# A graph-attention kernel: other PSUM grouping, later row sums of squares, three adjacency tiles turned early, and PE busy until x comes

## The chip, the cores and the metric

The kernel runs on one core of one Trainium2 chip. The time is the device time of one execution in microseconds. Before the change it is 2200.85 us, the median of 3 runs (2199.65 to 2201.54). The profiled execution spans 2198.8 us.

## The reference

There are 16 images (B) of 1024 nodes (N) with 256 channels (C), and one adjacency matrix of 1024 x 1024 for all. All is float32. Cut to what matters:

```python
fea = transpose(x, (0, 2, 1)); c_adj = mean(fea, axis=1)              # a mean per node
diff = c_adj[:, None, :] - c_adj[:, :, None]
A = abs(abs(sigmoid(diff) - 0.5) - 0.5) * 2.0                         # likeness of two nodes
g = relu(einsum('bcn,bnm->bcm', fea, adj * (A + A^T) / 2) * para)     # queries: a graph product
k, v = x @ kv_w                                                       # keys, values, 4 heads of 64
x = layernorm(x + softmax(q k^T * scale) v)
h = relu(x @ w1_loop + adj @ (x @ w1_neigh) + b1)                     # two graph convolutions
h = relu(h @ w2_loop + adj @ (h @ w2_neigh) + b2)
x = layernorm(x + (x + h) / 2)
```

## The kernel before

One function writes the order of the work by hand, engine by engine: within `tc.manual_schedule()` each engine runs its instructions in the order in which `run()` (L834) calls them, and waits only where a tile is not yet written, or where a buffer is still in use. Image by image, `run()` overlaps four things: the attention of image b, the query graph of image b+1, and the two graph convolutions of images b-1 and b-2.

**Attention** (L495). Four units (two pairs of heads, two halves of the nodes). `scores` makes eight tiles of 128 x 1024 with PE, takes the exponential of each on ScalarE (ACT, L519) and adds the eight up on VectorE (DVE, L525). `outputs` multiplies them with the values; `add` divides and adds the result onto x in a blocked layout (`xB`).

**Query graph.** For the first two images, `Queries` (L367) loads a row of adjacency tiles, weighs it by the likeness (two ACT passes, one DVE pass) and runs eight steps of plain matmuls. From the third image on, `FastQueries` (L410) makes the 2 x 2 block product from seven products instead of eight. `step` (L456) runs over four k; at k = 0 it takes three PSUM tiles of two banks each ("big") and one bank, and gives the seven sums their places: products 1 and 6 share tile a, 7 and 5 tile b, 2 and 3 tile c, and 4 has the single bank. In the last step they are finished in the order 1, 6, 2, 7, 4, 5, 3. `end` (L475) combines them: ACT copies product 1 (L482), then DVE makes seven additions (L483 to L489), two multiplications by para (L491), and ACT two relus (L492).

**Keys and values** of the next image follow on PE at once: `keys` (L342) takes two big PSUM tiles, one after the other, and ACT copies each to kT (L352); `values` (L355) takes four single banks in turn, and ACT copies each to v (L364). There are three big tiles and two single banks in all, and scores use the big ones as well. Between the two halves of the keys stands one small matmul (L256) that sums the squares over channels, for the variance.

**The norm after attention** is `BlockedNorm` (L301). `mean` subtracts the mean of each node (L312), `squares` squares on ACT (L318), sums over 32 channels on DVE (L319) and joins the two halves (L260). `variance` (L322) makes the small matmul, scales on DVE (L324) and takes the power -1/2 on GpSimd (L326). `scale` (L328) and `spread` (L333) multiply and transpose on DVE and store the nodes. In the steady image the calls are: step 2 of the query graph, with `mean` and `squares` inside it, step 3, `end`, the keys with `variance` between their halves, `scale`, `spread`, the values.

**The transposed adjacency.** The convolutions need the transposed matrix. `adj_blocked` (L204) loads a tile in blocks of 32 x 32 with four DMAs of small pieces, and `turn_adj` (L864) transposes it in two halves on DVE (L871) into tiles that stay in SBUF, or, for the upper right quarter, into row buffers (`rows01`) that are stored to DRAM later. All eight tiles are loaded and turned within image 1's query graph (b = 0). Row buffers (`row_tile`, L99) are 23 of 128 x 1024, shared by nearly everything.

**The start.** x of image 0 is loaded in four pieces; `prepare_first` (L219) transposes them on PE as they come (L227), then follow the keys, a row of means, the values, and the query graph of image 0, whose fifth step (t = 4) also prepares image 1 on DVE: its transposes and the sums for its means.

Of the kernel before, what the change touches and what calls it, by code (L numbers as in the profile page):

```python
# [18 lines left out]
def kernel(  # L19
# [31 lines left out]
    nc = tc.nc  # L51
# [39 lines left out]
    def bank_psum(name):  # L91
        return psum.tile([P, FB], F32, tag="bank", name=name, bufs=2)
# [6 lines left out]
    def row_tile(name):  # L99
        return work.tile([P, N], F32, tag="row", name=name, bufs=ROWS)  # L100

    def load_blocked(b, name):
        tiles = []
        for cc in range(NC):
            t = row_tile(f"xB_{name}_{cc}")
            for a in range(Q):
                c0 = cc * P + a * S
                nc.sync.dma_start(
                    out=t[a * S:(a + 1) * S, :].rearrange("k (bn r) -> k bn r", r=S),
                    in_=x[b, :, c0:c0 + S].rearrange("(bn k) r -> k bn r", k=S))  # L110
            tiles.append(t)
        return tiles
# [185 lines left out]
    def by_node(t):  # L298
        return t.rearrange("p (bn r) -> p bn r", r=S)

    class BlockedNorm:  # L301
# [10 lines left out]
                nc.vector.tensor_sub(x_cc, x_cc, mean.unsqueeze(2).to_broadcast([P, NB, S]))  # L312

        def squares(self):
            self.part = small.tile([P, NC, NB], F32, tag="part", name=f"sq_part_{self.name}", bufs=2)
            for cc in range(NC):
                sq = row_tile(f"sq_{self.name}_{cc}")
                nc.scalar.activation(sq, self.xB[cc], AF.Square)  # L318
                nc.vector.tensor_reduce(self.part[:, cc, :], by_node(sq), AX.X, ALU.add)  # L319
            join(self.part)  # L320

        def variance(self):  # L322
# [44 lines left out]
    class Queries:  # L367
# [35 lines left out]
        def end(self):  # L403
            qT = work.tile([P, NC, N], F32, tag="qT", name=f"qT_{self.b}")
            for cb in range(NC):
                nc.vector.tensor_mul(qT[:, cb, :], self.pg[cb], para_sb[:, cb, :])
                nc.scalar.activation(qT[:, cb, :], qT[:, cb, :], AF.Relu, scale=QSCALE)  # L407
            return qT

    class FastQueries(Queries):  # L410
# [45 lines left out]
        def step(self, k, halfway=None):  # L456
            if k == 0:
                a, b, c = (big_psum(f"g_ps_{self.b}_{i}") for i in range(3))
                h0, h1 = ts(0, FB), ts(1, FB)
                self.p = {1: a[:, h0], 6: a[:, h1], 7: b[:, h0], 5: b[:, h1], 2: c[:, h0], 3: c[:, h1],  # L460
                          4: bank_psum(f"g_ps_{self.b}_3")}
            lo, hi = self.wg.pop(k), self.wg.pop(TJ + k)
            t12, t4 = self.T.pop(k)
            h0, h1 = ts(0, FB), ts(1, FB)
            terms = {1: (self.block(0, 0), lo[:, h0]), 2: (self.block(0, 1), hi[:, h0]), 3: (self.S[3], hi[:, h1]),
                     4: (self.block(1, 1), t4), 5: (self.S[0], t12[:, h0]), 6: (self.S[1], t12[:, h1]),
                     7: (self.S[2], lo[:, h1])}

            for n in (1, 6, 2, 7, 4, 5, 3) if k == TJ - 1 else (1, 2, 3, 5, 7, 6, 4):
                if n == 7 and halfway:  # L470
                    halfway()
                x_n, w_n = terms[n]
                nc.tensor.matmul(self.p[n], x_n[:, k, :], w_n, start=(k == 0), stop=(k == TJ - 1))  # L473

        def end(self):  # L475
            qT = work.tile([P, NC, N], F32, tag="qT", name=f"qT_{self.b}")
            u = row_tile(f"U_{self.b}")
            h0, h1 = ts(0, FB), ts(1, FB)
            p = self.p
            add = nc.vector.tensor_add  # L480
            p1 = row_tile(f"P1_{self.b}")[:, h0]
            nc.scalar.copy(p1, p[1])  # L482
            add(u[:, h0], p1, p[6])  # L483
            add(qT[:, 0, h0], p1, p[2])
            add(u[:, h1], u[:, h0], p[7])
            add(qT[:, 1, h0], u[:, h1], p[4])
            add(qT[:, 1, h1], u[:, h1], p[5])
            add(u[:, h0], u[:, h0], p[5])
            add(qT[:, 0, h1], u[:, h0], p[3])  # L489
            for cb in range(NC):  # L490
                nc.vector.tensor_mul(qT[:, cb, :], qT[:, cb, :], para_sb[:, cb, :])  # L491
                nc.scalar.activation(qT[:, cb, :], qT[:, cb, :], AF.Relu, scale=QSCALE)  # L492
            return qT

    class Attention:  # L495
# [46 lines left out]
        def add(self, u):  # L542

            b, (pair, j) = self.b, UNITS[u]
            half = FB // S
            pd = bank_psum(f"den_ps_{b}_{u}")
            den = pd[:, 0:2 * half]
            nc.tensor.matmul(den, fold.rearrange("p a k -> p (a k)"), self.part.pop(u), start=True, stop=True)
            rden = small.tile([P, half], F32, tag="rden", name=f"rden_{b}_{u}", bufs=2)
            for s in range(2):  # L550
                rows = slice(s * HD, (s + 1) * HD)
                nc.vector.reciprocal(rden[rows, :], den[rows, ts(s, half)])
            nc.vector.tensor_tensor(den_min, den_min, den, ALU.min)
            nc.vector.tensor_tensor(den_max, den_max, den, ALU.max)
            o = by_node(self.o.pop(u))
            nc.vector.tensor_mul(o, o, rden.unsqueeze(2).to_broadcast([P, half, S]))
            dst = by_node(self.xB[pair][:, ts(j, FB)])
            nc.vector.tensor_add(dst, dst, o)
            nc.vector.tensor_reduce(self.sums[:, pair, ts(j, half)], dst, AX.X, ALU.add)
            if u == len(UNITS) - 1:  # L560
                join(self.sums)
# [272 lines left out]
    def run():  # L834
# [3 lines left out]

        xT, c_col = prepare_first(x_first)
        q = Queries(0, x_first)
        for t in range(NT):
            q.load(t)
        load_para()
        blocked = load_blocked(1, "1")
        load_weights()

        def first_weights():
# [7 lines left out]
        for t in (1, 2):  # L857
            q.times_adj(t)
        xb = load_x(1, "1")
        tiles = {}  # L860

        rows01 = []

# [9 lines left out]
        for t in range(NT):  # L873
            if t + 3 < NT:
                q.weigh(t + 3)
            q.step(t)
            if t == 4:
                xB = load_blocked(0, "a0")
                ready = {}
                ready["xT"], ready["part"] = prepare(blocked, "1")  # L880
            if t == 6:
                ready["mean"] = means(ready["part"], "1")
        qT = q.end()
        convs = {}
        for b in range(B):
# [84 lines left out]
            if more and not c1:  # L970
                xT = ready["xT"]
                for t in range(3, NT):
                    q.load(t)
                for t in range(3, NT):
                    q.likeness(t)
                for mt in range(4):
                    tiles[mt] = adj_blocked(mt)
                q.times_adj(3)
                q.step(0)
                q.times_adj(4)  # L980
                q.step(1)
                att.add(3)
                for mt in range(4, NT):
                    tiles[mt] = adj_blocked(mt)
                q.times_adj(5)
                q.step(2)
                q.step(3)
                norm.mean()
                q.times_adj(6)
                q.times_adj(7)  # L990
                q.step(4)
                norm.squares()
                q.step(5)
                q.step(6)
                norm.variance()
                xB = load_blocked(b + 1, f"a{b + 1}")
                q.step(7)
                qT = q.end()
                norm.scale()
                norm.spread()  # L1000
                turn_adj(range(NT))
                kT, v = keys(b + 1, xT), values(b + 1, xT)
            elif more:
                xT = ready["xT"]
                q.pair(2)
                q.step(0)
                q.step(1, lambda: att.add(3))
                q.pair(3)
                q.step(2, lambda: (norm.mean(), norm.squares()))
                q.step(3)  # L1010
                qT = q.end()
                xB = load_blocked(b + 1, f"a{b + 1}")
                kT = keys(b + 1, xT, norm.variance)
                norm.scale()
                norm.spread()
                v = values(b + 1, xT)
            else:
                c2.load_h1()
                c2.load_x()
                both.fetch(2, 3)  # L1020
                c1.inner()
                both.left(nc.gpsimd)
                both.fetch(1, 4)
                both.run({1: (lambda: att.add(3),), 2: (norm.mean, norm.squares), 7: (norm.variance,),
                          5: (norm.scale, norm.spread)})
                c1.turn(0)
                c2.last()
                c1.turn(1)
# [85 lines left out]
```

## Time and profile before

| what | value |
|---|---|
| time, median of 3 | 2200.85 us |
| span of the profiled execution | 2198.8 us |
| PE busy | 2172.8 us (99%) |
| DVE busy | 1864.0 us (85%) |
| ACT busy | 969.3 us (44%) |
| GpSimd busy | 328.1 us (15%) |
| DMA moved | 258.59 MB, mean 118 GB/s |
| mean granted TensorE clock | 0.997 |
| one image in the steady part | some 134.7 us |

Busy shares say what an engine did, not what it cost; idle time of an engine that nobody waits for costs nothing. In the timeline a row has the start in us, the length in us, the engine, the line, the operation, and what it writes and reads; several equal instructions in a row are merged, with their number after the x. In brackets stands the idle time of the engine before it and what ended it. In the waits, a row has the waiting engine and line, what it waited for, and the total, the number and the longest wait. A matmul of the program shows as two records on PE. PE is TensorE, PEld its weight loads.

### The profile page before, as it was taken

What the parts mean: (1) busy time and instruction counts of PE and PEld (TensorE: products, weight loads), DVE (VectorE), ACT (ScalarE), POOL (GpSimd) and SP (SyncE); (2) the same over time, 40 slices, a digit from 0 to 9 for tenths busy, and PEclk for the clock granted to TensorE, in tenths of its full rate; (3) what the DMA queues carried; (4) which work ended last, traced back from release to release, by engine and by line L of the source; (5) the groups of instructions that cost most, each with busy time, mean ns of one, the idle gap of its engine ahead of it and who ended that gap; (6) DMA issues with size and microseconds to landing.
All of it is one profiled execution on the core that took longest, in us unless ns stands there. A gap on an engine that the chain in (4) does not pass through costs nothing.

```text
span 2198.8 us, 22720 instructions
## 1 busy us (share of the span) xinstructions
PE 2172.8 (99%) x8096; PEld 1032.4 (47%) x8096; DVE 1864.0 (85%) x2453; ACT 969.3 (44%) x1064; POOL 328.1 (15%) x177
## 2 busy tenths in 40 slices
PE   8998999999999999999999999999999999999997
PEld 4344444544444444444444445445454444544354
DVE  4988888888898988988889788998989889888965
ACT  4734445434454443545444454434544445434511
POOL 1000020210302103021030301203012020210021
PEclk9999999999999999999999999999999999999999
DMA  8294372633646335463453734527264272733342
GB/s 193 86 139 148 60 182 68 124 125 63 177 100 151 104 58 172 96 172 88 75 162 78 182 86 78 172 58 182 86 92 157 58 182 88 137 114 64 116 134 97
DMA packets 586359, 258.59 MB, mean 118 GB/s; under 512 B 488064, under 2 KB 552448, under 8 KB 586240
## 3 DMA queue, kind: packets, MB, share of 16 engines
q1 hardware_dynamic: 585968, 256.56, 48.4%
q8 instruction: 65, 1.06, 0.2%
q14 instruction: 54, 0.44, 0.1%
q10 hardware_dynamic: 272, 0.52, 0.1%
HBM read 210.90 MB, written 46.14 MB: 117 GB/s over the span
## 4 chain that ended last, share of the span: by engine, by line
PE 72%; DVE 24%; issue 2%; ACT 1%; DMA 0%; DVEq 0%; SPq 0%; POOLq 0%; ACTq 0%; POOL 0%
PE hu_ps L793 16%; PE s L516 15%; PE av L536 15%; DVE acc L525 6%; PE k_ps L350 5%; PE v_ps L362 5%; PE t_ps L634 3%; PE h_ps L700 2%; PE hu_ps L641 2%; PE g_ps L400 2%; PE h_ps L701 2%; DVE wg L392 2%; DVE sq_part L319 1%; DVE wg L446 1%; DVE T L445 1%
## 5 line engine op out<-in xcount | busy, mean ns | idle before, releaser
L519 ACT ACTIVATE pr<-s 128x1024 f32<-128x1024 f32 x512 | 476.1, 1052 | 179.5 <-PE s L516 179.1
L525 DVE TENSOR_TENSOR acc<-acc,pr 128x1024 f32<-128x1024 f32 x384 | 493.2, 1285 | 41.4 <-DVE acc L525 0.9
L516 PE MATMUL s<-qT,kT 64*128 64x512 f32 x2048 | 457.2, 596 | 0.7 <-ACT qT L407 0.7
L536 PE MATMUL av<-pr,v 128*64 128x512 f32 x2048 | 453.6, 595 | 0.0
L516 PEld LDWEIGHTS s<-qT,kT 64*128 64x128 f32 x2048 | 190.9, 186 | 236.5 <-ACT pr L519 114.8
L536 PEld LDWEIGHTS av<-pr,v 128*64 128x64 f32 x2048 | 141.4, 137 | 300.0 <-issue 289.7
L326 POOL TENSOR_TENSOR rstd<-rstd,neg_half 128x32 f32<-128x32 f32 x16 | 87.1, 5441 | 1149.9 <-DVE rstd L324 1149.9
L386 ACT ACTIVATE wg<-c_row,c_col 128x1024 f32<-128x1024 f32 x128 | 147.1, 1149 | 86.5 <-DVE accB L527 50.6
L392 DVE SCALAR_TENSOR_TENSOR wg<-wg,adj 128x1024 f32<-128x1024 f32 x128 | 149.9, 1211 | 10.4 <-ACT wg L387 10.4
L793 PE MATMUL hu_ps<-adj,R 128*128 128x512 f32 x360 | 158.3, 596 | 0.0
L387 ACT ACTIVATE wg<-wg 128x1024 f32<-128x1024 f32 x128 | 135.4, 1058 | 4.1
L350 PE MATMUL k_ps<-xT,kvw_sb 128*128 128x512 f32 x256 | 117.9, 605 | 2.9 <-DVE U L483 2.8
L318 ACT ACTIVATE sq<-xB_a 128x1024 f32<-128x1024 f32 x32 | 33.8, 1057 | 192.4 <-DVE xB_a L312 178.8
L473 PE MATMUL g_ps<-wg,S 128*128 128x512 f32 x224 | 116.7, 603 | 0.0
L473 PE MATMUL g_ps<-T,S 128*128 128x512 f32 x224 | 114.4, 592 | 0.0
L362 PE MATMUL v_ps<-kvw_sb,xT 128*128 128x256 f32 x512 | 113.1, 379 | 0.0
L331 DVE TENSOR_TENSOR xB_a<-xB_a,rstd 128x1024 f32<-128x1024 f32 x32 | 38.8, 1255 | 84.4 <-POOL rstd L326 84.4
L473 PE MATMUL g_ps<-wg,x 128*128 128x512 f32 x224 | 109.0, 599 | 0.0
L362 PEld LDWEIGHTS v_ps<-kvw_sb,xT 128*128 128x128 f32 x512 | 97.3, 190 | 20.1 <-issue 7.7
L523 DVE TENSOR_TENSOR acc<-pr,pr 128x1024 f32<-128x1024 f32 x64 | 78.1, 1220 | 33.8 <-ACT pr L519 33.8
L793 PE MATMUL hu_ps<-adjT,t 128*128 128x512 f32 x240 | 105.7, 592 | 0.0
L793 PEld LDWEIGHTS hu_ps<-adj,R 128*128 128x128 f32 x360 | 67.3, 190 | 78.9 <-issue 75.8
(167 smaller groups left out, 2718.7 us busy)
## 6 DMA issues: line engine op xcount, KB each, us to landing
adj<-in_adj_dram SPq DMA_DIRECT2D x128, 512.0 KB, 4.5
adj<-adjT SPq DMA_DIRECT2D x120, 512.0 KB, 7.5
xB_a<-in_x_dram SPq DMA_DIRECT2D x128, 128.0 KB, 4.1
x1d<-xB_a SPq DMA_DIRECT2D x128, 128.0 KB, 3.4
x<-x1d SPq DMA_DIRECT2D x16, 1024.0 KB, 6.8
xB<-in_x_dram SPq DMA_DIRECT2D x120, 128.0 KB, 4.6
x<-in_x_dram SPq DMA_DIRECT2D x15, 1024.0 KB, 7.0
out_dram<-x SPq DMA_DIRECT2D x15, 1024.0 KB, 4.6
```

What stands on the lines that cost most here:

```text
L326: nc.gpsimd.tensor_tensor(self.rstd, self.rstd, neg_half, ALU.pow)
L350: nc.tensor.matmul(pk[:, ts(j, FB)], kvw_sb[:, cc, ts(kb, P)], xT[:, cc, ts(j, FB)], start=(cc == 0), stop=(cc == NC - 1))
L362: nc.tensor.matmul(pv[:, ts(i, C)], xT[:, cc, ts(g * per + i, P)], kvw_sb[:, cc, C:2 * C], start=(cc == 0), stop=(cc == NC - 1))
L386: nc.scalar.activation(wg, self.c_row, AF.Abs, bias=self.c_col[:, t:t + 1], scale=-1.0)
L387: nc.scalar.activation(wg, wg, AF.Tanh, scale=-0.5)
L392: nc.vector.scalar_tensor_tensor(wg, wg, 1.0, self.adj.pop(t), op0=ALU.add, op1=ALU.mult)
L473: nc.tensor.matmul(self.p[n], x_n[:, k, :], w_n, start=(k == 0), stop=(k == TJ - 1))
L516: nc.tensor.matmul(ps[:, ts(s, FB)], self.kT[rows, pair, ts(mt, P)], self.qT[rows, pair, ts(j, FB)], start=True, stop=True)
L519: nc.scalar.activation(pr, ps, AF.Exp)
L525: nc.vector.tensor_add(acc, acc, pr)
L536: nc.tensor.matmul(pav[s * HD:(s + 1) * HD, :], self.v[:, mt, pair * P + s * HD:pair * P + (s + 1) * HD], self.pr[mt][:, ts(s, FB)], start ...
L793: nc.tensor.matmul(dst, self.x[n][:, k, :], half_adj[w][:, k, :] if w else of_rows(rows, k), start=(start and k == 0), stop=(k == TJ - 1), ...
```

## The change

There are four edits.

1. Other PSUM grouping: product 2 joins 7 in tile b, and 5 joins 3 in tile c, so that tiles come free in the order in which the additions use them: a after the first addition, b after the third.
2. The row sums of squares leave `squares` and become `sum_squares`. In the steady image it is called in the middle of `end`, behind the third addition, so that the first three additions, which free PSUM tiles, do not stand behind the sums on DVE. In the other two places it follows `squares` as before.
3. Three of the eight adjacency tiles are loaded at the start, before the weights of the convolutions, and turned in the query graph of image 0 (t = 4, after image 1 was prepared). The other five stay where they were.
4. Sixteen transposes of the identity into a PSUM bank that nobody reads keep PE busy while x is on its way.

```diff
         def squares(self):
+            self.sq = [row_tile(f"sq_{self.name}_{cc}") for cc in range(NC)]
+            for cc in range(NC):
+                nc.scalar.activation(self.sq[cc], self.xB[cc], AF.Square)
+
+        def sum_squares(self):
             self.part = small.tile([P, NC, NB], F32, tag="part", name=f"sq_part_{self.name}", bufs=2)
             for cc in range(NC):
-                sq = row_tile(f"sq_{self.name}_{cc}")
-                nc.scalar.activation(sq, self.xB[cc], AF.Square)
-                nc.vector.tensor_reduce(self.part[:, cc, :], by_node(sq), AX.X, ALU.add)
+                nc.vector.tensor_reduce(self.part[:, cc, :], by_node(self.sq[cc]), AX.X, ALU.add)
             join(self.part)
...
-                self.p = {1: a[:, h0], 6: a[:, h1], 7: b[:, h0], 5: b[:, h1], 2: c[:, h0], 3: c[:, h1],
+                self.p = {1: a[:, h0], 6: a[:, h1], 2: b[:, h0], 7: b[:, h1], 5: c[:, h0], 3: c[:, h1],
                           4: bank_psum(f"g_ps_{self.b}_3")}
...
-        def end(self):
+        def end(self, between):
...
             add(u[:, h1], u[:, h0], p[7])
+            between()
             add(qT[:, 1, h0], u[:, h1], p[4])
...
+        idle = bank_psum("idle")
+        for _ in range(16):
+            nc.tensor.transpose(idle[:, 0:P], ident, ident)
         xT, c_col = prepare_first(x_first)
...
         blocked = load_blocked(1, "1")
+        tiles = {mt: adj_blocked(mt) for mt in range(3)}
         load_weights()
...
-        tiles = {}
...
                 ready["xT"], ready["part"] = prepare(blocked, "1")
+                turn_adj(range(3))
...
-                for mt in range(4):
-                    tiles[mt] = adj_blocked(mt)
+                tiles[3] = adj_blocked(3)
...
                 norm.squares()
+                norm.sum_squares()
...
-                turn_adj(range(NT))
+                turn_adj(range(3, NT))
...
-                qT = q.end()
+                qT = q.end(norm.sum_squares)
...
-                both.run({1: (lambda: att.add(3),), 2: (norm.mean, norm.squares), 7: (norm.variance,),
+                both.run({1: (lambda: att.add(3),), 2: (norm.mean, norm.squares, norm.sum_squares), 7: (norm.variance,),
```

## The prediction

> **What bounds the kernel now.** I read the page's busy shares and its chain first, then who waits for whom on PE, then the timeline of each engine around the places the change touches.
>
> ```profile
> PE 2172.8 (99%) x8096; PEld 1032.4 (47%) x8096; DVE 1864.0 (85%) x2453; ACT 969.3 (44%) x1064; POOL 328.1 (15%) x177
> ...
> PE 72%; DVE 24%; issue 2%; ACT 1%; DMA 0%; DVEq 0%; SPq 0%; POOLq 0%; ACTq 0%; POOL 0%
> ```
>
> PE has work nearly always, so only PE's idle time can be won, and any new PE wait is paid in full. The waits of PE are few:
>
> ```profile
> PE den_ps L548 <- DVE o L540: 5.6, 1, 5.6
> PE xT_ps L227 <- DMA x<-in_x_dram: 4.9, 2, 4.7
> PE k_ps L350 <- DVE U L483: 2.8, 13, 0.5
> ```
>
> One is at the start (x not there yet), one is single (image 1), and one comes back at each of the 14 images whose query graph is the seven-product form. Here is one of these 14 on ACT, DVE and PE (timeline from 394.4 us; start, length, instruction):
>
> ```profile
> 394.47 2.19 ACT L318 ACTIVATE sq<-xB_a 128x1024 f32<-128x1024 f32 x2 [12.44 <-DVE xB_a L312]
> 396.57 0.57 ACT L482 COPY P<-g_ps 128x512 f32<-128x512 f32 x1
> 403.88 2.19 ACT L492 ACTIVATE qT<-qT 128x1024 f32<-128x1024 f32 x2 [6.74 <-DVE qT L491]
> 405.98 1.91 ACT L352 COPY kT<-k_ps 128x1024 f32<-128x1024 f32 x2
> 407.91 0.58 ACT L364 COPY v<-v_ps 128x512 f32<-128x512 f32 x1
> ...
> 395.56 2.35 DVE L319 TENSOR_REDUCE sq_part<-sq 128x32 f32<-128x1024 f32 x2
> 398.06 0.68 DVE L483 TENSOR_TENSOR U<-P,g_ps 128x512 f32<-128x512 f32 x1
> 399.26 0.68 DVE L485 TENSOR_TENSOR U<-U,g_ps 128x512 f32<-128x512 f32 x1
> 402.62 2.36 DVE L491 TENSOR_TENSOR qT<-qT,para_sb 128x1024 f32<-128x1024 f32 x2
> ...
> 397.60 1.02 PE L473 MATMUL g_ps<-wg,S 128*128 128x512 f32 x2
> 398.79 3.70 PE L350 MATMUL k_ps<-xT,kvw_sb 128*128 128x512 f32 x8 [0.17 <-DVE U L483]
> 405.99 7.07 PE L362 MATMUL v_ps<-kvw_sb,xT 128*128 128x256 f32 x32
> ```
>
> See three things. DVE has no gap from 395.56 on. The keys' first matmul waits for L483, since it takes the PSUM tile that L483 reads last: the two matmuls from 397.60 take 0.43 us each, so the keys could start at 398.46 and start at 398.79, 0.33 us late, plus 0.10 us to refill (8 matmuls take 3.54 us to the next instruction at 402.33, not 8 x 0.43). And the chain behind L491 is serial: relu (L492), copies of kT, copy of v. That copy frees the bank of the third group of values.
>
> **What the skill says.** "TensorE: Matmul & The Clock Gate", section on the array of 32x32 sub-arrays, has ScalarE and VectorE as strict first-in-first-out, with only weight loads pulled ahead on PE; the lines agree, as ACT idles 6.74 us before L492 with the kT copies queued behind it. The same page, Part 1 on the clock gate, says that an idle PE runs at half clock until some 3.4 us of activity lie in a free-running window. The trace agrees: transposes at the start take 0.213 us each, later ones 0.109, and the change comes 5.3 us after the first. "DMA: Bandwidth & Descriptors", on small descriptors, has a fixed overhead per packet; the blocked loads (128-byte pieces) move some 140 GB/s here against some 410 GB/s for full rows.
>
> **Part 1, PSUM grouping and the squares behind the third addition (14 times).** No instruction is added or removed; products 7, 5 and 2 swap places in two PSUM tiles, and on DVE two reductions and a join move from ahead of L483 to behind L485.
> - Gain. L483 then waits only for ACT's copy P, which ends at 396.57 + 0.57 = 397.14. It starts at 397.17 instead of 398.06, ends before 397.9, and the keys start at 398.46: 0.33 + 0.10 = 0.43 us per image.
> - The new wait. DVE stands idle from the mean's subtraction (ended 395.51) to 397.17, where it used to reduce. The reductions and join (395.56 to 398.06: 2.50 us) now come after L485. Fourth addition: 397.17 + 1.20 (L483 to L485) + 0.60 (an addition whose result the next does not read) + 2.50 = 401.47, where before it was 399.98: 1.49 us later. Everything on DVE behind it is 1.49 us later: L491 at 404.11, and rstd (404.89, now 406.4).
> - Does that reach PE? The sum matmul (L256), due at 398.46 + 3.44 = 401.90, needs the join, which ends at about 401.55: just in time, nothing. The second half of the keys takes the tile with products 2 and 7, free at 399.1: nothing. The second group of values needs rstd's bank at 407.3; rstd ends at 406.6: nothing. The third group needs the first copy of v. ACT in order: relu at 405.37, kT at 407.47, v at 409.40 to 409.98. PE would get there at 405.99 - 0.43 + 2 x 1.73 = 409.02 (1.73 us is a group: copies of v start 1.73 us apart further on). It waits until 409.98 + 0.05 (L483's end to PE's start is 0.05 in the trace), so 410.03. Before, it was there at 409.45 without a wait, with the copy done at 408.49, 0.96 us of room. So 0.58 us late, plus 0.10 for the refill: 0.68 us per image, net of the gain.
> - Behind that PE is busy without a gap through the image, so it stays lost. DVE's own lag (1.49, against PE's 0.68) lands in its idle stretch before the first accumulation of the scores, 0.81 us in the first such image, so no more is lost there.
> - Sum: 14 x 0.68 = +9.5 us. The bounds on each are 0.4 (no refill, shorter wait) and 0.9.
>
> **Part 2, PE busy until x comes.** Sixteen transposes of the identity, 0.213 us each, from about 1.5 us (DVE reads the identity at 1.50) to 4.9. x's first transposes begin at 4.73 now and at 4.9 then, but the next batch waits for data until 5.99 anyway, so that costs nothing.
>
> ```profile
> 4.73 1.09 PE L227 MATMUL xT_ps<-ident,x 128*128 128x128 f32 x4 [4.73 <-DMA x<-in_x_dram]
> ...
> 8.60 4.29 PE L350 MATMUL k_ps<-xT,kvw_sb 128*128 128x512 f32 x8
> ```
>
> If full clock comes 5.3 us after the first transpose again, it comes at 6.8: of the twelve from 5.99 on, four are done, eight save 0.104 us each and the keys' first matmuls 4.13 - 3.44 = 0.69. That is 1.5; c_col on DVE, ready about 11.3 (copies of xT until 8.6, then reductions of 2.33 and a scaling of 0.17 us) and needed when the keys end at 11.15, leaves 1.4. The window's phase makes it 0.7 to 1.6: -1.4 us. PE runs without a wait from there to the first scores, so it stays.
>
> **Part 3, three adjacency tiles early.** 12 load issues and 6 transposes of 0.60 us (16 take 9.57) move from image 1's turn into image 0's graph. On DVE they meet 9.11 us idle before the mean (L265). The loads queue behind xB (issued until 24.6) at some 1.0 us each (32 such in 32.26 us later on) to 1.4 (the last six of xB in 8.29) and take 4.5 us to land: landed at 41 to 46, transposed by 43 to 47; the mean comes at about 46.9. So 0, at worst +0.5. Where they are removed, DVE waits for others:
>
> ```profile
> 145.45 9.57 DVE L871 STREAM_TRANSPOSE adjT<-adjB 128x512 f32<-128x512 f32 x16
> 155.37 1.22 DVE L523 TENSOR_TENSOR acc<-pr,pr 128x1024 f32<-128x1024 f32 x1 [0.36 <-ACT pr L519]
> ...
> 170.33 0.52 DVE L552 RECIPROCAL rden<-den_ps 64x16 f32<-64x16 f32 x2 [2.60 <-PE den_ps L548]
> ...
> 190.28 0.64 PE L548 MATMUL den_ps<-den_part,fold 128*128 128x32 f32 x2 [5.56 <-DVE o L540]
> ```
>
> The additions at 155.37 already wait for ACT, and the chain that ends in PE's 5.56 us starts at 170.33, released by PE itself. So the 3.6 us bring nothing: 0. Two row buffers are held longer for rows of the transposed adjacency, which moves image 1's first loads from 67 to about 81 us; they are used from 100.1 us on, so 0. Weights and x of image 1 issue some 12 to 17 us later, and are needed after 110 us: 0.
>
> Sum: 2200.85 + 9.5 - 1.4 = 2209.0 us.
>
> **Rivals.**
> - B, faster. The values' third group doesn't wait, since ACT catches up. For it: 0.96 us of room now. Against it: four copies and relus in one queue, all of it behind L491. 14 x 0.43 + 1.4 = 7.4 us less: 2193.4.
> - C, gain and loss cancel. DVE's lag is only some 1.0 us (reductions pipelined tighter, or additions that used to wait for each other). Then the third group comes about 0.2 us late per image: 2.8 - 1.4, 2202.
> - D, worse. The lag of rstd, scaling and transposes isn't absorbed at the next image's accumulation, where the room equals the lag (0.81 against 1.49 - 0.68). Up to 0.8 us more per image: +11, 2220.
>
> **How the numbers follow.** A, the sum above, 0.58 (2205 to 2212); B 0.17; C 0.14; D 0.11. The threshold is 4.4 us. Faster is B and a sliver: 0.18. Same is C and a little: 0.16. Slower is the rest of A and D: 0.66. The range takes in A, most of C and the nearer half of D: 2198 to 2215.
>
> **What would show it.** In the profile after: k_ps no longer waiting for U; a new wait of v_ps for ACT's copy of v, about 1.0 us, 14 times; L483 on DVE with some 1.6 us of idle before it, put down to ACT's P; transposes of 0.109 us before 8 us; den_ps in image 1 still waiting 5.6 us. I am wrong if v_ps shows no wait, if the 5.6 us shrink, or if a load in image 0 holds up the mean.

## The result, and the profile after

The changed kernel takes 2213.69 us (median, 2212.32 to 2214.86), the kernel before 2200.98 us. The ratio is 1.0058 with a 95% interval of 1.0045 to 1.0071: slower, by 12.7 us. The forecast was slower, by 8.2 us, with a range to 2215.

The page after, busy shares and chain:

```profile
PE 2178.5 (98%) x8112; PEld 1036.4 (47%) x8112; DVE 1865.5 (84%) x2453; ACT 966.6 (44%) x1064; POOL 327.4 (15%) x177
...
PE 51%; DVE 35%; SPq 5%; ACT 3%; issue 3%; DMA 2%; POOL 1%; DVEq 0%; ACTq 0%; POOLq 0%
```

DVE does the same work (1865.5 us against 1864.0), and yet its share of the chain went from 24 to 35%. More telling is what is new in the chain: the sync queue (SPq) with 5% and DMA with 2%, both 0% before. The prediction speaks of neither in the steady images.

Who waits for whom, PE first:

```profile
PE v_ps L365 <- ACT v L367: 10.1, 14, 0.9
PE den_ps L552 <- DVE o L544: 5.6, 1, 5.6
PE den_ps L552 <- DVE den_part L533: 3.1, 5, 0.8
...
PE mean_ps L256 <- DVE o L544: 1.5, 7, 0.2
```

The wait of the keys for U is gone, and the predicted wait of the values for ACT's copy is there 14 times. The 5.6 us in image 1 haven't moved. The third and the last line are the surprise: waits in the second stretch of an image (the first convolution's products), for DVE. And on DVE itself:

```profile
DVE U L486 <- ACT P L485: 23.2, 14, 1.7
DVE xT L216 <- DMA xB<-in_x_dram: 6.4, 7, 1.3
```

The first line is the idle stretch that was predicted. The second was not: in 7 images DVE waits for the next image's blocked x, which in the profile of the kernel before was always there.

The image shown before, now (timeline from 396 us; line numbers are 3 or 4 higher):

```profile
407.05 2.19 ACT L496 ACTIVATE qT<-qT 128x1024 f32<-128x1024 f32 x2 [8.20 <-DVE qT L495]
...
410.94 1.08 ACT L367 COPY v<-v_ps 128x512 f32<-128x512 f32 x2
...
398.88 0.69 DVE L486 TENSOR_TENSOR U<-P,g_ps 128x512 f32<-128x512 f32 x1 [1.66 <-ACT P L485]
...
403.17 0.68 DVE L490 TENSOR_TENSOR qT<-U,g_ps 128x512 f32<-128x512 f32 x1
...
405.79 2.36 DVE L495 TENSOR_TENSOR qT<-qT,para_sb 128x1024 f32<-128x1024 f32 x2
...
407.27 3.62 PE L365 MATMUL v_ps<-kvw_sb,xT 128*128 128x256 f32 x16
411.59 3.72 PE L365 MATMUL v_ps<-kvw_sb,xT 128*128 128x256 f32 x16 [0.70 <-ACT v L367]
```

Counted from the end of ACT's copy P to the first scores, this stretch takes 16.40 us in each image, where it took 15.85: 0.55 us lost, 14 times. That leaves some 5 us to be found.

They are in the sync queue. The next two fences are its timeline behind this point, before (first scores of the image at 412.99 us) and after (at 415.25 us):

```profile
411.88 6.36 SPq L339 DMA_DIRECT2D x1d<-xB_a  x8
...
421.13 10.85 SPq L108 DMA_DIRECT2D xB<-in_x_dram  x8
```

```profile
415.06 6.21 SPq L342 DMA_DIRECT2D x1d<-xB_a  x8
...
423.46 11.92 SPq L108 DMA_DIRECT2D xB<-in_x_dram  x8
```

The queue issues without a pause, and starts when DVE has scaled the first half (L334). Against the first scores that is 1.11 us ahead of them before and 0.19 us ahead after: 0.92 us later. The eight loads of the blocked x stand at the end of the same queue, and their last issue ends 18.99 us behind the first scores before and 20.13 us after. On DVE this comes out as

```profile
437.11 1.23 DVE L216 STREAM_TRANSPOSE xT<-xB 128x1024 f32<-128x1024 f32 x1
439.14 1.25 DVE L216 STREAM_TRANSPOSE xT<-xB 128x1024 f32<-128x1024 f32 x1 [0.81 <-DMA xB<-in_x_dram]
```

In both kernels the second of these transposes is due 23.02 us behind the first scores. In these two traces, where the last issue of the loads ended up to 19.6 us behind the first scores (all images before), it started within 0.05 us of that; where the issue ended later (8 of 13 images after), it started 0.2 to 1.5 us late. What PE lost by it is seen in the time from one image's first scores to the next's; six of the images after (the first four of the 14, the eleventh and the twelfth), worked out from the starts in the timeline:

| last load issued, us behind first scores | second transpose late, us | image longer than 135.25 us by |
|---|---|---|
| 20.73 | 1.51 | 1.41 |
| 20.13 | 0.88 | 0.79 |
| 20.00 | 1.30 | 1.22 |
| 19.35 | 0.01 | 0.00 |
| 19.83 | 0.79 | 0.70 |
| 20.73 | 1.50 | 1.42 |

PE pays nearly all of it, since DVE has no idle time in the second stretch to make it good. Summed over the 13 distances between images: 13 x 0.53 = 6.9 us from 134.72 to 135.25, and 7.4 us of longer images, of which 1.0 us was there before, so 6.4. The first of the 14 images has its first scores 0.3 us later than before (278.58 against 278.27 us): its own 0.55 lost, and of the 1.0 us that the start had won only some 0.2 is left by then (see the idle transposes below). 6.9 + 6.4 + 0.3 = 13.6 us; the two profiled executions differ by 13.5, the medians by 12.7.

### The profile page after: what moved, and what is told of

Same layout as the page of the kernel before. It is cut to its first block, busy times and chain, and to the rows that moved or that the text cites. A ratio compares the mean times of both kernels' runs of the same rounds, so it can differ in the third digit from the quotient of the medians.

```text
span 2212.3 us, 22722 instructions
## 1 busy us (share of the span) xinstructions
PE 2178.5 (98%) x8112; PEld 1036.4 (47%) x8112; DVE 1865.5 (84%) x2453; ACT 966.6 (44%) x1064; POOL 327.4 (15%) x177
## 4 chain that ended last, share of the span: by engine, by line
PE 51%; DVE 35%; SPq 5%; ACT 3%; issue 3%; DMA 2%; POOL 1%; DVEq 0%; ACTq 0%; POOLq 0%
PE hu_ps L797 14%; PE s L520 11%; PE av L540 10%; DVE acc L529 9%; SPq L108 3%; PE h_ps L704 2%; PE g_ps L403 2%; PE h_ps L705 2%; DVE wg L395 2%; PE v_ps L365 2%; PE hu_ps L645 2%; DVE qT L495 1%; POOL rstd L329 1%; DVE sq_part L322 1%; DMA xB<-in_x_dram 1%
## 5 line engine op out<-in xcount | busy, mean ns | idle before, releaser
L334 DVE TENSOR_TENSOR xB_a<-xB_a,rstd 128x1024 f32<-128x1024 f32 x32 | 38.8, 1254 | 84.4 <-POOL rstd L329 84.4
```

## Experiments

**One edit at a time.** The first two edits (grouping, and sums behind the third addition) belong together, so they are one kernel; the grouping alone, the tiles alone and the idle transposes alone are three more. Their edits are the hunks of the diff above.

Edits 1 and 2:

> The kernel before with the first two edits alone: the PSUM grouping, and the row sums of squares behind the third addition. Theory: everything that the change lost is here, so +13 to +14 us against the kernel before (the measured +12.7 and the 1.0 us that the start won), with the v_ps wait for ACT's copy of v (about 10 us in 14) and DVE's wait for the blocked x (about 6 us in 7) as in the changed kernel. Rival (the three early tiles shift buffers and so the loads of the blocked x): about +6.5 us, 14 x 0.54 less a little, and DVE never waits for the blocked x.

2212.57 us against 2201.41: ratio 1.0049 [1.0032, 1.0066], +11 us. That is less than the expected 13 to 14, which its interval (7 to 14.5) takes in. PE waits for v 10.5 us in 14, DVE for the blocked x 4.6 us in 8. So both losses come with these two edits, and neither needs the tiles.

Edit 3, the tiles:

> The kernel before with the third edit alone: three adjacency tiles loaded and turned in image 0's query graph. Theory: 0 (within 1 us), PE's single wait of den_ps for o stays at 5.6 us, and DVE doesn't wait for the blocked x. Rival (the tiles shift buffers and make the blocked x late): +5 to +7 us and DVE waits for the blocked x in about half of the images.

2201.13 us, ratio 0.9999 [0.9990, 1.0007]: nothing, with the single wait at 5.6 us still. A part of the expectation missed: DVE waited for the blocked x after all, 2.8 us in 4. So these loads were at the edge already, and a profile that shows no wait isn't a proof of room: the kernel before shows none, and its latest loads ended at 19.6 us. Such waits show in the traces of the idle transposes alone (1.3 us in 3) and of the grouping alone (0.5 us in 3) as well, so it isn't shown that the tiles cause them.

Edit 4, the idle transposes:

> The kernel before with the fourth edit alone: sixteen transposes of the identity while x is on its way. Theory: -1.0 us (the first scores of image 0 come 1.0 us earlier in the changed kernel's trace, 51.48 against 52.49 us), and nothing later gives it back. As I had predicted it: -1.4. Rival (lost again in image 1): 0.

2201.2 us, ratio 0.9997 [0.9988, 1.0006]. The trace shows the first scores at 51.43 us instead of 52.49; the interval is too wide (-2.6 to +1.3 us) to say how much of that reaches the end. In this trace nothing does: the first of the 14 images has its first scores at 278.32 us, in the kernel before at 278.27. The gain is lost behind PE's wait of 5.6 us in image 1. In both traces TensorE's granted clock stands at half for 6.8 us there, but PE, back from its wait, works through 6.26 us of it with the idle transposes and through 4.03 us before, and reaches its next scores after 20.67 us instead of 19.57. This stretch takes from 19.1 to 20.8 us in the traces that leave its order as it was, whichever edit they have, so the traces don't say what is left of the gain on average. The expectation's rival (lost again in image 1) stays open.

The start itself varies too. Without the edit, the row of means comes at anything from 11.79 to 13.41 us. When x lands is only a part of that: its second batch is transposed from 5.99 us on in the kernel before and from 6.03 on with the tiles alone, and the means come at 12.73 and at 11.89. With the edit they come at 11.40 to 11.89.

Edit 1, the grouping:

> The kernel before with the PSUM grouping alone, the sums of squares left where they were. Theory: 0 (within 0.5 us): the keys' first half still waits 0.33 us for the first addition, which stands behind the sums on DVE, and the keys' second half, due at 402.4 us in the image looked at, finds its tile free in both groupings (before: the sixth addition ended at 401.86). Rival (the grouping itself costs or brings something): more than 1 us either way.

2201.79 us, ratio 1.0004 [0.9995, 1.0013]: nothing, and the keys wait as before (2.5 us in 13).

**Sums without the grouping.** The kernel before, with edit 2 alone.

> The kernel before with the sums of squares behind the third addition, but the PSUM grouping left as it was. Theory: the keys' second half takes the tile of products 7 and 5, which only the sixth addition frees; that ended 405.04 in the changed kernel's image, where the second half is due at 403.62, so a new wait of k_ps for U of about 1.4 us, 14 times, and the v_ps wait (1.0 us) goes, since PE gets there later: 14 x (1.5 - 0.43) = +15 us, less what the loads of the blocked x gain on a later PE: +10 to +18. Rival (the grouping has no part in it): +11 with the v_ps wait of 10 us, as with both edits.

2231.18 us, ratio 1.0137 [1.0120, 1.0155]: +30 us, far more than expected. Its waits (PE, then DVE):

```profile
PE k_ps L353 <- DVE U L492: 19.4, 14, 1.4
...
DVE qT L487 <- PE g_ps L476: 10.8, 14, 0.9
```

The first wait is the expected one, to the size. The last line was not foreseen: the second addition reads product 2, which shares a tile with product 3 in the old grouping, and product 3 is the last to be finished. The addition waits 0.77 us for it, and all behind it is late by that, the join too, for which PE's sum matmul now waits 6.0 us in 14. An image without further losses takes 136.55 us, 1.83 more than before, where 1.07 was expected; this wait is the difference. 14 x 1.83 makes 26 of the 30 us; the trace also has late loads (2.9 us in 7) and one stretch of 3.4 us at half clock. So the grouping is what makes early additions possible at all, and my prediction, which saw in it only when tiles come free for the keys, had missed this half.

**Stores off the sync queue.** The changed kernel with

```diff
-        def spread(self):
+        def spread(self, aside=False):
...
-                    nc.sync.dma_start(out=nodes[:, c0:c0 + S].rearrange("(bn k) r -> k bn r", k=S),
+                    (nc.gpsimd if aside else nc.sync).dma_start(out=nodes[:, c0:c0 + S].rearrange("(bn k) r -> k bn r", k=S),
...
-                norm.spread()
+                norm.spread(True)
```

> The changed kernel with one thing moved: the eight stores of the normalised nodes (x1d) are issued by GpSimd in the steady images, so that the sync queue no longer waits for DVE's scaling before it can issue the next image's blocked x. Theory (the lag of DVE is carried past its idle stretch by the in-order queue: late stores, late loads, DVE waits): DVE's wait for the blocked x (6.4 us in 7) goes, PE's waits of den_ps for den_part and of mean_ps for o go with it, the v_ps wait stays at 10 us; 5 to 6.5 us less than the changed kernel, so +6 to +8 against the kernel before. Rival (DVE simply stays late, whatever the loads do): the time stays at +12 to +13 against the kernel before.

2206.85 us, ratio 1.0023 [1.0014, 1.0032], +5.3 us, 6.8 less than the change (7.4 when each is held against the kernel before as measured beside it). Its waits:

```profile
PE v_ps L365 <- ACT v L367: 10.1, 14, 0.9
...
PE den_ps L552 <- DVE den_part L533: 0.8, 1, 0.8
```

The second transpose starts at 23.02 us behind the first scores in every image, the means (mean_ps) wait no more, and the v_ps wait is untouched. DVE scales as late as in the changed kernel; only the loads come earlier. So the rival (DVE simply stays late) falls. The control, the same move in the kernel before:

> A control: the kernel before, with only the stores of x1d issued by GpSimd in the steady images, as in the run that took 6.8 us off the changed kernel. Theory (the sync queue matters only because the changed kernel's stores are late): within 1.5 us of the kernel before. Rival (these stores are better off on GpSimd in any kernel): -4 to -7 us.

2201.11 us, ratio 0.9999 [0.9990, 1.0008]. The move is worth something only where the stores are late.

**A dose of lateness.** The kernel before, with two stores more in the sync queue behind x1d:

```diff
-        def spread(self):
+        def spread(self, more=0):
...
+            for k in range(more):
+                spare = dram.tile([N, S], F32, tag=f"spare{k}", name=f"spare{k}_{self.name}", bufs=3)
+                nc.sync.dma_start(out=spare.rearrange("(bn k) r -> k bn r", k=S), in_=by_node(self.xB[1][96:128, :]))
...
-                norm.spread()
+                norm.spread(2)
```

> The kernel before with two extra stores of 32 columns each into a spare tensor behind the eight stores of x1d in the steady images: the sync queue is some 1.5 us later at the next image's blocked x (a store takes it 0.8 us), nothing else is changed. In the changed kernel the same loads end 1.1 us late. Theory: with no change on any compute engine, DVE now waits for the blocked x in at least half of the images and PE loses behind it: +5 to +12 us, with no v_ps wait. Rival (late loads are no cause, DVE's own lag is): within 1 us of the kernel before.

2228.62 us, ratio 1.0118 [1.0101, 1.0135], +27 us, more than expected.

```profile
PE den_ps L551 <- DVE den_part L532: 17.4, 13, 2.4
...
DVE xT L216 <- DMA xB<-in_x_dram: 21.8, 14, 2.5
```

The two issues take 2.73 us in the image looked at, where I had put 1.5. Late loads alone, with no compute instruction changed and no v_ps wait, are enough to make PE wait in the second stretch. (The two stores also move data; what that adds to the lateness was not separated.)

PE lost more than DVE waited. The trace is of the slowest of the four executions, 2235.42 us, some 34 us above the kernel before, and it shows a second cost. Behind five of PE's waits, each of 1.7 to 2.0 us, the granted clock falls to half for 3.4 us. Here are one of these waits with the 24 matmuls behind it, and then the same 24 matmuls in an image at full clock:

```profile
866.75 0.41 PE L551 MATMUL den_ps<-den_part,fold 128*128 128x32 f32 x2 [1.73 <-DVE den_part L532]
867.61 12.24 PE L796 MATMUL hu_ps<-adj,R 128*128 128x512 f32 x24
...
459.44 10.55 PE L796 MATMUL hu_ps<-adj,R 128*128 128x512 f32 x24
```

Five stretches of 3.4 us at half clock cost some 8.5 us. The mean granted clock is 0.993 in this execution and 0.994 to 0.995 in the other three, against 0.997 in the kernel before. So the +27 us are not the price of the late loads alone.

**The second relu out of the way.** The changed kernel with ACT's relu of the second half of the queries behind the copies of the values:

```diff
-                nc.scalar.activation(qT[:, cb, :], qT[:, cb, :], AF.Relu, scale=QSCALE)
+                if cb == 0:
+                    self.cut(qT, cb)
...
+        def cut(self, qT, cb):
+            nc.scalar.activation(qT[:, cb, :], qT[:, cb, :], AF.Relu, scale=QSCALE)
...
                 v = values(b + 1, xT)
+                q.cut(qT, 1)
```

> The changed kernel with ACT's second relu (channels 128 to 255 of the queries, not needed before the third unit of scores) moved behind the copies of the values. Theory: kT and v are copied 1.1 us earlier, so the v_ps wait (1.0 us, 14 times) goes; but PE then runs ahead of a DVE that is as late as before, so that part of the 14 us comes back as waits behind DVE (the first additions of the scores start with no slack, the blocked x comes no earlier): between -4 and -10 us against the changed kernel. If the v_ps wait were all that counts: -14 us. If the wait only hides DVE's lag: 0.

2210.42 us, ratio 1.0043 [1.0026, 1.0059]: some 3 us less than the change by the medians, just short of the range; but the four executions lie from 2206.28 to 2212.15, which doesn't settle whether it falls short. The trace is of the fastest. In it the v_ps wait is gone, but DVE's wait for the blocked x grew from 6.4 us in 7 to 10.0 us in 12, and PE's for den_part from 3.1 to 4.0. PE is earlier against the same late stores. The wait had cost some 14 us (14 x 0.98); 7.8 of them come in at the end in this execution, 3 by the medians. Removing a wait on PE while its cause, DVE's lag, stays, moved about half of the loss, or more, to the next place.

**Split sums.** The changed kernel, but with one half of the sums left ahead of the additions, where DVE is idle, and P copied between the two squares:

```diff
+        def sum_square(self, cc):
...
+            nc.vector.tensor_reduce(self.part[:, cc, :], by_node(self.sq[cc]), AX.X, ALU.add)
+            if cc == 1:
+                join(self.part)
...
-        def end(self, between):
+        def end(self, first, between):
...
             nc.scalar.copy(p1, p[1])
+            first()
             add(u[:, h0], p1, p[6])
             add(qT[:, 0, h0], p1, p[2])
             add(u[:, h1], u[:, h0], p[7])
             between()
...
-                q.step(2, lambda: (norm.mean(), norm.squares()))
+                q.step(2, lambda: (norm.mean(), norm.square(0), norm.sum_square(0)))
...
-                qT = q.end(norm.sum_squares)
+                qT = q.end(lambda: norm.square(1), lambda: norm.sum_square(1))
```

> The changed kernel with the sums split: square and sum of the first half of the channels ahead of the additions, ACT's copy of product 1 between the two squares, the second sum and the join behind the third addition. DVE then has work while product 1 is copied, and the additions 4 to 7 come when they came in the kernel before. Theory (what costs is the idle 1.66 us on DVE and the lag that it makes): no k_ps wait, no v_ps wait, no wait for the blocked x; 14 x 0.43 = 6 us and the start's 1.0 us less than the kernel before: -7, about 2194. Rival (PE ahead by another 0.43 us finds the third group of values or the den_ps wait instead): -1 to -2 us.

2193.94 us against 2201.52, ratio 0.9966 [0.9953, 0.9978]: 7.6 us faster than the kernel before, as the theory had it. The same stretch of DVE:

```profile
393.94 1.22 DVE L330 TENSOR_REDUCE sq_part<-sq 128x32 f32<-128x1024 f32 x1
395.07 0.68 DVE L496 TENSOR_TENSOR U<-P,g_ps 128x512 f32<-128x512 f32 x1
...
396.87 1.21 DVE L330 TENSOR_REDUCE sq_part<-sq 128x32 f32<-128x1024 f32 x1
```

The two additions left out stand between at 0.60 us each, so there is no gap: P is ready 0.57 us behind the first square instead of behind both, and the first sum fills the time. An image takes 134.28 us instead of 134.72, which is the 0.43 us of the keys' wait, and PE's share of the chain is 97%. PE's waits for the tiles of the keys and of the values are gone, and DVE waits for the blocked x once, 0.2 us.

The same split alone on the kernel before, with the old grouping, no tiles and no idle transposes:

> The kernel before with only the split sums (first half ahead of the additions, product 1 copied between the two squares, second half behind the third addition): old PSUM grouping, no early tiles, no idle transposes. Theory: the sixth addition ends at about 401.9 as before, and the keys' second half is now due at about 402.04, so the old grouping just does: -5 to -6.5 us, about 2195.5. Rival (the grouping is needed): the second half waits for the sixth addition, and -2 us or less.

2211.71 us, ratio 1.0048 [1.0031, 1.0065]: 10 us slower. My expectation failed, and by the cause that the sums without the grouping show:

```profile
396.08 0.68 DVE L496 TENSOR_TENSOR U<-P,g_ps 128x512 f32<-128x512 f32 x1
398.05 0.69 DVE L497 TENSOR_TENSOR qT<-P,g_ps 128x512 f32<-128x512 f32 x1 [1.29 <-PE g_ps L485]
...
402.54 3.70 PE L362 MATMUL k_ps<-xT,kvw_sb 128*128 128x512 f32 x8 [0.95 <-DVE U L502]
```

The second addition waits 1.29 us, until the last matmul of the query graph (396.99, two of them, ending 398.01) is through, although product 2, which it reads, is finished third of the seven. The sixth addition is late by it, and the keys' second half waits 0.95 us for that one's tile. (The tiles and the idle transposes, by which the two kernels differ too, changed nothing that could be measured alone.) So of the change, the grouping is worth keeping, and it is the placing of the sums that lost the time.

**Image 1.** Split sums, and PE given the first half of a convolution in place of the 5.6 us:

```diff
-        def first(self, rows01):
+        def first(self, rows01, between=lambda: None):
             for j in range(NJ):
+                if j:
+                    between()
...
-                    att.add(1)
-                    for t in (0, TJ):
-                        q.likeness(t)
-                    store("01", rows01)
-                    adj_sums(rows01)
-                    weigh_first()
-                    c1.first(rows01)
+                    def rest():
+                        att.add(1)
+                        for t in (0, TJ):
+                            q.likeness(t)
+                        store("01", rows01)
+                        adj_sums(rows01)
+                        weigh_first()
+
+                    c1.first(rows01, rest)
```

> The changed kernel with split sums, and in image 1 the first half of the first convolution moved on PE ahead of the denominators of the second unit, where PE waits 5.6 us for DVE. DVE has no idle time from 172 to 207 us there, and 2.7 us in the waits just behind it. Theory: DVE bounds that stretch, so 0 to -3 us against the run with split sums alone (2193.9). Rival (PE's wait is a matter of order alone): -5.6 us.

2196.06 us, ratio 0.9975 [0.9964, 0.9985], no better than the split alone. PE no longer waits 5.6 us there, and waits 7.3 us at the denominators of the third unit instead: DVE bounds that stretch, and PE's wait only moves. Behind it the granted clock is at half for 10.2 us in this trace, and 32 matmuls of scores take 9.67 us, where the 32 of the unit before take 7.14.

## Why the prediction was right, and where it was not

**Right, with its sizes: the chain from the additions to the values.** From the start of the first addition, the prediction had the fourth addition 4.30 us later (measured 403.17 - 398.88 = 4.29), the multiplication 6.94 (6.91), the relu 8.20 (8.17), the first v copied after 12.81 (12.66, since ACT's copies ran 0.1 us tighter). From PE's first matmul of the values to the first scores it took 7.00 us before (405.99 to 412.99) and takes 7.98 now (407.27 to 415.25), so the wait with its refill costs 0.98, where 1.11 was forecast; the gain ahead of it is the forecast 0.43. Net per image 0.68 was predicted, 0.55 measured: 14 x 0.55 = 7.7 instead of 9.5. With the loads out of play this is about what the stores on GpSimd measured: +5.3, where 7.7 - 1.0 = 6.7 was due, inside its interval (3.1 to 7.0).

**Wrong: "DVE's own lag (1.49, against PE's 0.68) lands in its idle stretch before the first accumulation of the scores, 0.81 us in the first such image, so no more is lost there."** For DVE this was so. The first accumulation starts 3.14 us behind the first scores in both kernels, and the idle 0.86 us ahead of it is used up. But the scaling stands ahead of that idle stretch, and the sync queue takes its start from the scaling. The queue, in order and without a pause for some 20 us, carries the lag of 0.92 us past the place where DVE had made it good, and hands it back to DVE as late loads. This cost 6.4 us in the profile, and 6.8 in the run that took the stores off the queue. The prediction looks at no wait of the sync queue; in the kernel before, "SPq L339 <- DVE xB_a L331" is its largest wait.

The forecast of +8.2 us held against +12.7 only because its range took in the nearer half of rival D: the prediction's own sum, A, ended at 2212, and 2213.69 lies past it. That the loss of 9.5 us came out at 7.7 hid a part of the missing 6.4, which is luck.

**Rival D** had about this much more loss (up to 0.8 us an image) for another reason, an accumulation that starts late. The size was near, the reason was not: the loss sits in the images whose loads were late, from nothing to 1.4 us, and goes when only the stores move.

**The start.** Full clock comes as predicted: four of the twelve transposes from 6.22 us on are still done at half clock, the other eight and the keys run at full (3.60 us for the keys' first eight matmuls instead of 4.29). The first scores come 1.0 us earlier, not 1.4, in part because x's second batch landed 0.23 us later in this profile than in that of before. "So it stays" was too much, though: behind the wait of image 1 PE works 5.63 us at half clock in this trace, where it was 4.03 before, which takes 0.8 us back. The runs don't resolve the gain at the end of the kernel.

**The tiles** brought nothing, as costed, and the 5.6 us stayed.

**Rivals B and C** fell with the v_ps wait. What B wanted, the keys early and no lag, is what the split sums do: 2193.94 us, where B had 2193.4.

## What to carry to other kernels

When an instruction moves on an in-order engine, follow what it delays to the DMA issues that wait for it, and then to everything queued behind those issues: a lag that the engine itself makes good in its next idle time can come round again through the queue. To let urgent instructions pass, move only so much of the other work as doesn't leave the engine idle: half of the sums filled the gap that moving all of them had opened. When PE gets a new wait, look at the granted clock behind it too: in the dose of lateness, a wait of under 2 us was at times followed by 3.4 us at half clock. And group sums in PSUM tiles by when they are finished as well as by when they are read.

## What was not expected of the hardware

An addition that reads one half of a two-bank PSUM tile started only after the last matmul into the other half: some 1.3 us of waiting in each of 14 images with split sums and the old grouping, none with the new. It was shown that the wait goes with the grouping; in the built program the addition's wait counts up to product 3's last matmul, so it is the program that asks for it, tile by tile; whether the memory would have allowed less was not tried. Further, the margin of the blocked loads is narrower than a profile without waits lets one think: in the traces of before and after, loads issued by 19.6 us behind the first scores cost nothing, and for those issued by 20.7 us DVE waits up to 1.5 us. The border isn't sharp: with the tiles alone, one image's loads, issued by 19.56 us, came 0.5 us late and another's, issued by 19.79, in time. Eight stores moved to GpSimd kept it busy for 98 us more in 112 stores, 0.87 us each, which cost the kernel before nothing.

PE's short waits can cost more than their length. In the dose of lateness the clock fell to half for 3.4 us behind five of the six waits of 1.7 us or more (the one of 2.37 us was not followed by it) and behind none of the four from 0.7 to 1.5 us. In the kernel before with the sums alone it did so once in 14 waits of 1.4 us. What decides between them was not tried.
